# Buffers held until their transfer has landed, a dearer change of array shape, an early table load and an output per tile, in a kernel whose order is planned in Python

## The chip, the cores and the metric

The kernel runs on one core of a Trainium2 chip. The metric is the device time of one execution, in microseconds (us). Before the change the median of three runs is 1993.94 us (1992.65 to 1994.4). One more execution was profiled: it took 1996.48 us, of which the profile's span covers 1994.7 us. Lines such as L372 are lines of the kernel before.

## What is computed

The input is x of shape (4, 1024, 256), float32. It is normalised, and two branches of the normalised xn are added to it:

```python
xn = layernorm(x)
x + attention(xn) + ffn(xn)

# attention: 16 heads of 64, window 64, each query block sees its own and the previous block of keys
h = rms_norm(xn) * gamma
q, k, v = h @ W_qkv                      # 256 -> 3 * 1024
o = softmax(mask(q @ k.T / 8)) @ v
attention = (o * sigmoid(h @ W_gates + b_gates)) @ W_out

# ffn: two layers, 8 heads of 64, window 128
for l in range(2):
    q, k, v = shift_token(x) @ wqkv[l]   # 256 -> 3 * 512
    q, k = rotary(l2norm(q) * qs, l2norm(k) * ks)
    x = x + local_attention(q, k, v) @ wo[l]
    h = layernorm(shift_token(x)) @ w1[l] + b1[l]     # 256 -> 2 * 682
    a, g = split(h)
    x = x + (a * gelu(g)) @ w2[l] + b2[l]
```

shift_token moves the second half of the features one token down. All arithmetic is in float32.

## The kernel before, in words

**Blocks.** The 4096 tokens are cut into 16 blocks of 256 (two tiles of 128). `first_attention(n)` does the normalisation and the 16-head attention of block n, and stores xn (`carried[0]`) and x plus attention (`carried[2]`) to DRAM, L350. `layer(l, n)` fetches a block (L356), does one ffn layer for it, and stores the result for the next layer (L350), or, in the last layer, adds it up and writes the output (L1300). A `layer` is a generator in two halves: the attention half, and, after the `yield`, the feed-forward half, which is recorded `LAG` blocks later.

**The order.** Nothing is issued when it is written down. Each step is recorded with `op(...)`: the engines that could do it with an estimated time on each, a function that issues it, and the buffers that it reads (`r`), writes (`w`) or adds to (`a`). `Plan.run` then plays all recorded steps through a small model of five engines (PE for TensorE, DVE for VectorE, ACT for ScalarE, POOL for GpSimd, SP for the queue that issues most transfers), and `emit` issues them in the order that came out. So the order on every engine is fixed before the chip sees it, and each engine works through its own list strictly in turn. In the model:

- a step's result is ready after its time and a latency, `LAT` (or `lat`), and DVE and POOL times are stretched by `SLACK`;
- each engine picks the step with the smallest score, which is the step's place in the recorded order (`rank`, in us of PE work), plus `IDLE` times the time that the engine would stand idle for it, plus `TURN` where the step has another `mode` than the one before;
- a change of `mode` also takes `SWITCH` us. On PE the mode is the shape in which the 128 x 128 array is used: `full` (128 x 128), `rc` (64 x 64: the score matmuls L711 and L1001, and the second half of the layer's `ob`, L1095) and `c` (128 x 64: `oa`, L779, and the first half of `ob`, L1083). On ACT it is the function table: `exp` or `gelu`;
- steps more than `LOOK` us ahead of the oldest one that is not done are not considered.

**Buffers.** A buffer gets a slot when its first step is planned, out of 92 SBUF slots (`w`), 4 for the gelu (`g`), 40 small ones (`s`) and the 8 banks of PSUM (`ps`). When its last step is planned, the slot becomes free at that step's end plus 0.1 us (L188). For a transfer that end is the end of its issue on SP, not its landing. `spare` keeps some slots of a kind back from steps that run ahead. On the chip, the program's semaphores make the next writer of a slot wait until its last reader has really finished, whatever the plan assumed.

**What each line is.** L385 holds all transposes (by the identity); L584, L677 the first attention's v and q, k; L805 its output projection; L864 the layer's q, k, v; L1114 its output projection; L1246 and L1282 the up and down projections of the feed-forward half. L370 and L372 copy from PSUM to SBUF, on ACT or DVE. L543 normalises twice: `hn` on POOL, which feeds the transposes, and `xn` on DVE, which is stored. L567 scales hT by gamma on ACT, and is the first step there that needs a table. L728 and L1020 are the masked minima of the scores, L738 and L1030 the exponentials, L756 and L1045 the weights, L1259 the gelu, L1266 its product, L1290 the last addition. L932 is the rotation, L361 a power on POOL, L1220 the affine step of the second normalisation.

Of the kernel before, what the change touches and what calls it, by code (L numbers as in the profile page):

```python
# [8 lines left out]
AF = mybir.ActivationFunctionType  # L9
# [32 lines left out]
N_UNIT = 92  # L42
N_GE = 4
N_SMALL = 40
LAG = 3

# [11 lines left out]

class Op:
    __slots__ = (
        "us", "fn", "bufs", "fresh", "mode", "rank", "lat", "left", "ready", "users", "done",
        "start", "end", "eng", "name", "n",
    )


class Plan:
    LAT = {"PE": 0.25, "DVE": 0.3, "ACT": 0.3, "POOL": 0.3, "SP": 2.0}
    SLACK = {"DVE": 1.2, "POOL": 1.2}  # L70
    SWITCH = {"PE": 0.1, "ACT": 1.4}
    TURN = {"PE": 5.0, "ACT": 40.0}
    IDLE = 300.0
    LOOK = 200.0

    def __init__(self, slots, spare):
# [5 lines left out]
    def buf(self, kind):  # L82
        return Buf(kind)

    def op(self, us, fn, r=(), w=(), a=(), mode=None, lat=None, name=""):


        o = Op()
        o.us, o.fn, o.mode, o.lat, o.name = us, fn, mode, lat, name
        o.rank, o.n = self.rank, len(self.ops)  # L90
        if "PE" in us:
            self.rank += us["PE"]
        o.users, o.done, o.ready = [], False, 0.0
        deps = set()
        for b in r:
            deps.update(b.writers)
            b.readers.append(o)
# [12 lines left out]
        o.left = len(deps)  # L110
        self.ops.append(o)
        return o

    def run(self):
        engines = ("PE", "ACT", "DVE", "POOL", "SP")
        at = dict.fromkeys(engines, 0.0)
        mode = dict.fromkeys(engines)
        waiting = {e: [] for e in engines}

        def enter(o):  # L120
            for e in o.us:
                waiting[e].append(o)

        for o in self.ops:
            if not o.left:
                enter(o)
        oldest, out = 0, []

        def begins(o, front):

            need = {}
            for b in o.bufs:
                if b.t is None:
                    need[b.kind] = need.get(b.kind, 0) + 1
            t = o.ready
            for k, n in need.items():
                have = self.free[k]
                keep, slope, most = self.spare[k]
                age = o.rank - front
                if len(have) - n < (min(keep + slope * age, most) if age > 2.0 else 0):  # L140
                    return None
                t = max(t, sorted(f[0] for f in have)[n - 1])
            return t

        while len(out) < len(self.ops):
            while self.ops[oldest].done:
                oldest += 1
            front = self.ops[oldest].rank
            best = None
            for e in engines:  # L150
                picks = []
                for o in waiting[e]:
                    if o.rank > front + self.LOOK:
                        continue
                    t = begins(o, front)
                    if t is None:
                        continue
# [15 lines left out]
            t, _, e, o = best  # L173
            for other in o.us:
                waiting[other].remove(o)
            o.done, o.start, o.end, o.eng = True, t, t + o.us[e] * self.SLACK.get(e, 1.0), e
            at[e] = o.end
            mode[e] = o.mode or mode[e]
            for b in o.bufs:
                if b.t is None:  # L180
                    have = self.free[b.kind]
                    have.sort(key=lambda f: f[0])

                    k = max((i for i, f in enumerate(have) if f[0] <= t), default=0)
                    b.slot = have.pop(k)
                    b.t = b.slot[1]
                b.left -= 1
                b.end = max(b.end, o.end)  # L188
                if not b.left and b.slot is not None:
                    self.free[b.kind].append([b.end + 0.1, b.slot[1]])  # L190
            give = o.end + (self.LAT[e] if o.lat is None else o.lat)
            for u in o.users:
                u.ready = max(u.ready, give)
                u.left -= 1
                if not u.left:
                    enter(u)
            out.append(o)
        self.order = out
# [7 lines left out]
def layers_kernel(  # L206
# [38 lines left out]
            "s": [work.tile([P, 32], F32, name=f"s{n}") for n in range(N_SMALL)],  # L245
            "ps": [psum.tile([P, 512], F32, name=f"ps{n}") for n in range(8)],
        },
        {"w": (4, 0.15, 30), "g": (1, 0.0, 1), "s": (4, 0.05, 12), "ps": (1, 0.02, 3)},
    )
    op, buf = plan.op, plan.buf  # L250

# [1 line left out]
    def fixed(shape, name):  # L253
        return Buf(None, const.tile(shape, F32, name=name))
# [25 lines left out]
        return b.t[:, : k * m * n].rearrange("p (k m n) -> p k m n", k=k, m=m)  # L280

    load_x(0)
    ident = fixed([P, P], "ident")
    load(ident.t, ident_d, ident, eng="ACT")
    gam = fixed([P, NC], "gam")
# [2 lines left out]
    def unit(pieces, us=2.3):  # L288

        u = buf("w")  # L290
        for n, (to, m, of) in enumerate(pieces):

            def bring(e, to=to, m=m, of=of):
                nc.sync.dma_start(u.t[:, to : to + m], of)

            op({"SP": m / 465}, bring, a=(u,), lat=us, name="weights")
        return u


# [48 lines left out]
    def store(dst, src, n):  # L348
        op(
            {"SP": 1.1}, lambda e: nc.sync.dma_start(dst.t, src.t[:, : NT * DIM]),  # L350
            r=(src,), w=(dst,), name="store",
        )

    def fetch(src, b):
# [151 lines left out]
    def first_attention(n, before):  # L506
# [31 lines left out]
            w=(st,), name="scale",  # L538
        )

        def normal(e, to, at):
            for i in range(NT):
                {"DVE": nc.vector, "POOL": nc.gpsimd}[e].tensor_scalar(  # L543
                    v2(to, NT, DIM)[:, i, :], X()[:, i, :], st.t[:, 12 + 2 * i : 13 + 2 * i],
                    st.t[:, at + i : at + i + 1], ALU.subtract, ALU.mult,
                )
# [272 lines left out]
    def layer(l, n, before):  # L819
# [35 lines left out]
        for i in range(NT):  # L855
# [211 lines left out]
            def attend(e, po=po, sTs=sTs, vs=vs, vs_next=vs_next, vt=vt, vt_old=vt_old):  # L1067
# [164 lines left out]
        for m in range(NM):  # L1232
# [39 lines left out]
                op({"DVE": 0.405}, gated, r=(pf, ge, w["b_vec"]), w=(gT[-1],), name="gT")  # L1272
            else:
                op({"DVE": 0.405}, gated, r=(pf, ge, w["b_vec"]), a=(gT[m // 2],), name="gT")
        xo = buf("w")
        for i in range(NT):
            pz = buf("ps")

            def down(e, pz=pz, i=i):
                for m in range(NM):  # L1280
# [7 lines left out]
            op(  # L1288
                {"DVE": 0.345},
                lambda e, pz=pz, i=i: nc.vector.tensor_tensor(  # L1290
                    v2(xo, NT, DIM)[:, i, :], pz.t[:, :DIM], v2(rest, NT, DIM)[:, i, :], ALU.add
                ),
                r=(pz, rest), a=(xo,), name="xo",
            )
# [12 lines left out]
    for n in range(len(blocks)):  # L1307
        if n % NBLK == 0:
# [108 lines left out]
```

## Time and profile before

| What | Value |
|---|---|
| median of three runs | 1993.94 us |
| the profiled execution: time, span | 1996.48 us, 1994.7 us |
| DVE, ACT, POOL busy | 1213.1, 1097.5, 1085.6 us (61%, 55%, 54%) |
| PE weight loads | 1542.5 us (77%), beside the matmuls |
| DMA | 89.36 MB, mean 45 GB/s; 221 GB/s in the first 50 us |
| ACT table loads | 34, of 1283 ns each |
| granted TensorE clock, mean | 0.998 |
| matmul L864 (128 x 512), L1246 (128 x 256), transposes L385 | 593, 380, 275 ns each as modelled |

A row of the timeline reads: start in us, duration in us, engine, line, operation, output <- input, and in brackets how long the engine stood idle before, and what ended that. The duration of a matmul in the records is longer than the distance to the start of the next one, since matmuls overlap: a full-array matmul of 256 columns is 0.38 us long, and the next starts 0.216 us after it. So what a group of matmuls takes is read from its start to the start of the next group. The names in the rows lack buffer numbers: `w` is any SBUF slot, `ps` any bank, `c` a DRAM buffer of `carried`. An SPq row is the issue of a transfer.

### The profile page before, as it was taken

The numbers are of one execution on the slowest core, as the hardware profiler recorded it, in microseconds if no ns is written. First come the engines' busy times: TensorE is split into PE (matmuls) and PEld (weight loads), VectorE is DVE, ScalarE is ACT, GpSimd is POOL, SyncE is SP. The second block draws the span as 40 slices with busy tenths as digits, with TensorE's granted clock in tenths as the row PEclk, the third lists the DMA queues.
The fourth block names the chain that finished last, engine by engine and source line by source line (L and its number), as shares of the span: only waits on it lengthen the run. The fifth ranks groups of instructions, "written<-read, shape, count | busy, mean of one in ns | idle before, by whom it ended". The sixth has DMA issues, their size and how long they took to land.

```text
span 1994.7 us, 50683 instructions
## 1 busy us (share of the span) xinstructions
PE 1953.6 (98%) x18752; PEld 1542.5 (77%) x18752; DVE 1213.1 (61%) x4449; ACT 1097.5 (55%) x3409; POOL 1085.6 (54%) x1697
## 2 busy tenths in 40 slices
PE   7899999999999999999999999999999999999998
PEld 5788888888788677777777777777777777777787
DVE  4444444344344687668677686776767767677662
ACT  4455555446465575655556455564555655556552
POOL 5664456356343786546555475564745646556540
PEclk9999999999999999999999999999999999999999
DMA  7421112111211112301111011110111101111010
GB/s 220 113 54 39 38 44 65 38 44 34 59 34 39 30 31 52 88 20 31 41 28 31 24 49 36 41 37 26 48 39 33 46 22 49 31 41 28 20 28 19
DMA packets 69911, 89.36 MB, mean 45 GB/s; under 512 B 17772, under 2 KB 37792, under 8 KB 69664
## 3 DMA queue, kind: packets, MB, share of 16 engines
q1 hardware_dynamic: 68960, 85.91, 15.9%
q8 instruction: 148, 2.42, 0.5%
q14 instruction: 99, 0.81, 0.1%
q10 hardware_dynamic: 704, 0.21, 0.1%
HBM read 32.61 MB, written 16.78 MB: 25 GB/s over the span
## 4 chain that ended last, share of the span: by engine, by line
PE 91%; DVE 4%; ACT 2%; DMA 1%; issue 1%; POOL 1%; SPq 0%; DVEq 0%; ACTq 0%; POOLq 0%
PE ps L864 16%; PE ps L1246 14%; PE ps L677 11%; PE ps L385 11%; PE ps L1282 8%; PE ps L805 6%; PE ps L584 6%; PE ps L1114 5%; PE ps L1001 4%; PE ps L779 3%; PE ps L1083 3%; PE ps L711 3%; PE ps L1095 2%; DVE w L372 1%; ACT w L370 1%; DMA c<-w 1%
## 5 line engine op out<-in xcount | busy, mean ns | idle before, releaser
L370 ACT COPY w<-ps 128x512 f32<-128x512 f32 (+2 forms) x911 | 428.1, 500 | 600.6 <-PE ps L677 155.0
L372 DVE COPY w<-ps 128x256 f32<-128x256 f32 (+3 forms) x465 | 246.3, 539 | 240.3 <-PE ps L385 110.9
L932 POOL TENSOR_TENSOR w<-w,w 128x256 f32<-128x256 f32 x256 | 234.9, 943 | 284.1 <-ACT w L370 149.9
L864 PE MATMUL ps<-w,w 128*128 128x512 f32 x768 | 352.1, 593 | 1.6 <-DVE w L372 0.9
L1246 PE MATMUL ps<-w,w 128*128 128x256 f32 x1408 | 322.5, 380 | 7.2 <-DVE w L1266 7.2
L1045 POOL TENSOR_SCALAR w<-w,s 128x192 f32<-128x192 f32 x512 | 229.9, 468 | 158.5 <-DVE s L1039 156.5
L385 PEld LDWEIGHTS ps<-ident,w 128*128 128x128 f32 x2112 | 245.9, 141 | 87.4 <-issue 21.7
L385 PE MATMUL ps<-ident,w 128*128 128x128 f32 x2112 | 290.2, 275 | 13.8 <-POOL w L543 9.4
L1246 PEld LDWEIGHTS ps<-w,w 128*128 128x128 f32 x1408 | 260.4, 190 | 45.0 <-ACT w L370 12.0
L756 POOL TENSOR_SCALAR w<-w,s,s 128x128 f32<-128x128 f32 x512 | 223.7, 456 | 110.2 <-DVE s L746 110.0
L361 POOL TENSOR_TENSOR s<-s,mhalf 128x16 f32<-128x16 f32 (+2 forms) x112 | 233.1, 2085 | 76.7 <-DVE s L911 26.7
L1030 ACT ACTIVATE w<-w,s 128x192 f32<-128x192 f32 x512 | 226.0, 445 | 51.2 <-DVE s L1020 49.2
L864 PEld LDWEIGHTS ps<-w,w 128*128 128x128 f32 x768 | 138.3, 190 | 127.5 <-issue 108.7
L677 PE MATMUL ps<-w,w 128*128 128x256 f32 x1024 | 235.6, 380 | 0.0
L738 ACT ACTIVATE w<-w,s 128x128 f32<-128x128 f32 x512 | 197.6, 388 | 28.9 <-DVE s L728 28.9
L677 PEld LDWEIGHTS ps<-w,w 128*128 128x128 f32 x1024 | 188.9, 190 | 25.4 <-ACT w L370 0.8
L1020 DVE CUSTOM_DVE_ANT_0 w<-ps,mask_b,s 128x192 f32<-128x192 f32 x512 | 183.0, 411 | 23.7 <-PE ps L1001 20.2
L1259 ACT ACTIVATE g<-ps,b 128x256 f32<-128x256 f32 x192 | 90.4, 474 | 180.4 <-PE ps L1246 158.5
L728 DVE CUSTOM_DVE_ANT_0 w<-ps,mask_a 128x128 f32<-128x128 f32 x512 | 112.7, 286 | 119.6 <-PE ps L711 102.4
L1282 PE MATMUL ps<-w,w 128*128 128x256 f32 x768 | 171.6, 379 | 2.2 <-ACT w L1220 1.2
L1282 PEld LDWEIGHTS ps<-w,w 128*128 128x128 f32 x768 | 145.6, 190 | 34.5 <-issue 10.1
L1266 DVE SCALAR_TENSOR_TENSOR w<-ps,b,g 128x256 f32<-128x256 f32 x192 | 91.2, 480 | 83.5 <-ACT g L1259 77.0
(75 smaller groups left out, 2584.9 us busy)
## 6 DMA issues: line engine op xcount, KB each, us to landing
w<-w SPq DMA_DIRECT2D x248, 128.0 KB, 2.3
c<-w SPq DMA_DIRECT2D x48, 256.0 KB, 2.0
w<-c SPq DMA_DIRECT2D x48, 256.0 KB, 2.9
w<-in_L_attn_x_dram SPq DMA_DIRECT2D x16, 256.0 KB, 3.2
out_dram<-w SPq DMA_DIRECT2D x16, 256.0 KB, 2.2
w<-w SPq DMA_DIRECT2D x32, 112.0 KB, 2.2
w<-in_L_ffn_w_dram SPq DMA_DIRECT2D x26, 128.0 KB, 2.8
w<-in_L_ffn_wqkv_dram SPq DMA_DIRECT2D x12, 256.0 KB, 3.4
```

The source lines that it names most:

```text
L361: nc.gpsimd.tensor_tensor(dst, src, mhalf.t[:, : src.shape[1]], ALU.pow)
L370: nc.scalar.copy(dst(), src())
L372: nc.vector.tensor_copy(dst(), src())
L385: nc.tensor.transpose(o, i, ident.t)
L677: nc.tensor.matmul(pq.t[:, j * TB : (j + 1) * TB], W[c].t[:, p % GA * P : (p % GA + 1) * P], hT.t[:, c * TB : (c + 1) * TB], start=(c == 0 ...
L756: nc.gpsimd.tensor_scalar(s.t[:, at], s.t[:, at], sm.t[:, 2 * GA + u : 2 * GA + u + 1], gate.t[:, h : h + 1], ALU.mult, ALU.mult,)
L864: nc.tensor.matmul(p.t, y.t[:, at : at + P], w["wqkv"][m][c].t[:, :512], start=(c == 0), stop=(c == NC - 1),)
L932: nc.gpsimd.tensor_tensor(v2(rot, HB, D)[:, :, to], v2(raw[m], HB, D)[:, :, of], v3(sin, 4, 2, D)[:, ti % 4, m, to].unsqueeze(1).to_broadc ...
L1030: nc.scalar.activation(v2(s, 2, WB)[:, u], v2(s, 2, WB)[:, u], AF.Exp, bias=sm.t[:, u : u + 1], scale=-1.0, accum_out=sm.t[:, 2 + u : 3 + u],)
L1045: nc.gpsimd.tensor_scalar(v2(s, 2, WB)[:, u], v2(s, 2, WB)[:, u], sm.t[:, 4 + u : 5 + u], 1.0, ALU.mult, ALU.mult,)
L1246: nc.tensor.matmul(pf.t[:, n_ * TB : (n_ + 1) * TB], wt, d.t[:, c * TB : (c + 1) * TB], start=(c == 0), stop=(c == NC - 1),)
L1282: nc.tensor.matmul(pz.t[:, :DIM], gT[m // 2].t[:, at : at + P], v2(w["w2"][m // 2], 2, DIM)[:, m % 2, :], start=(m == 0), stop=(m == NM - 1),)
```

## The change

It changes numbers and rules of the plan, and three steps:

- a slot that a transfer reads becomes free when the transfer has landed (`give`), not at the end of its issue; stores are given 3.5 us to land; a weight piece is given at least 0.45 us of issue;
- `ob` leaves PE in mode `rc` (its new argument `out`), where the plan took it to leave in `c`;
- other weights: TURN for PE 5 to 30, for ACT 40 to 60; IDLE 300 to 400; LAT of DVE, ACT and POOL 0.3 to 0.4; SLACK 1.2 to 1.25; the slots kept back, of `w` and `ps`; LAG 3 to 4;
- a two-column exponential of zeros, `early`, is recorded ahead of all but the first load, so that ACT loads the `exp` table there;
- `hn` is made on DVE, ahead of `xn`;
- the last layer writes each tile of 128 tokens from a buffer of its own, as soon as it is added up.

```diff
-LAG = 3
+LAG = 4
...
-    LAT = {"PE": 0.25, "DVE": 0.3, "ACT": 0.3, "POOL": 0.3, "SP": 2.0}
-    SLACK = {"DVE": 1.2, "POOL": 1.2}
+    LAT = {"PE": 0.25, "DVE": 0.4, "ACT": 0.4, "POOL": 0.4, "SP": 2.0}
+    SLACK = {"DVE": 1.25, "POOL": 1.25}
     SWITCH = {"PE": 0.1, "ACT": 1.4}
-    TURN = {"PE": 5.0, "ACT": 40.0}
-    IDLE = 300.0
+    TURN = {"PE": 30.0, "ACT": 60.0}
+    IDLE = 400.0
...
+        o.out = out or mode
...
-            mode[e] = o.mode or mode[e]
+            mode[e] = o.out or mode[e]
+            give = o.end + (self.LAT[e] if o.lat is None else o.lat)
...
-                b.end = max(b.end, o.end)
+                b.end = max(b.end, give if e == "SP" else o.end)
                 if not b.left and b.slot is not None:
                     self.free[b.kind].append([b.end + 0.1, b.slot[1]])
-            give = o.end + (self.LAT[e] if o.lat is None else o.lat)
...
-        {"w": (4, 0.15, 30), "g": (1, 0.0, 1), "s": (4, 0.05, 12), "ps": (1, 0.02, 3)},
+        {"w": (4, 0.1, 30), "g": (1, 0.0, 1), "s": (4, 0.05, 12), "ps": (0, 0.02, 3)},
...
     load_x(0)
+
+    early = fixed([P, 2], "early")
+    op({"POOL": 0.1}, lambda e: nc.gpsimd.memset(early.t, 0.0), w=(early,))
+    op(
+        {"ACT": 1.4}, lambda e: nc.scalar.activation(early.t, early.t, AF.Exp), w=(early,),
+        mode="exp", name="early",
+    )
...
-            op({"SP": m / 465}, bring, a=(u,), lat=us, name="weights")
+            op({"SP": max(m / 465, 0.45)}, bring, a=(u,), lat=us, name="weights")
...
-            r=(src,), w=(dst,), name="store",
+            r=(src,), w=(dst,), lat=3.5, name="store",
...
-        op({"POOL": 1.0}, lambda e: normal(e, hn, 24), r=(xb, st), w=(hn,), name="hn")
-        op({"DVE": 0.66}, lambda e: normal(e, xn, 20), r=(xb, st), w=(xn,), name="xn")
+        op({"DVE": 0.66}, lambda e: normal(hn, 24), r=(xb, st), w=(hn,), name="hn")
+        op({"DVE": 0.66}, lambda e: normal(xn, 20), r=(xb, st), w=(xn,), name="xn")
...
                 {"PE": 1.8}, attend, r=(*sTs[0], *sTs[1], vt, vt_old, vs, vs_next), w=po, mode="c",
-                name="ob",
+                out="rc", name="ob",
...
-        xo = buf("w")
+        xo, xos = buf("w"), [buf("w") for _ in range(NT)]
...
+            xi, at = (xo, i) if l < DEPTH - 1 else (xos[i], 0)
...
+            if l == DEPTH - 1:
+                op(
+                    {"SP": 0.6},
+                    lambda e, i=i, xi=xi: nc.sync.dma_start(
+                        out[b, g * TB + i * P : g * TB + (i + 1) * P, :], xi.t[:, :DIM]
+                    ),
+                    r=(xi,), name="out",
+                )
         if l < DEPTH - 1:
             store(carried[l + 1][n], xo, n)
-        else:
-            op(
-                {"SP": 1.1},
-                lambda e: nc.sync.dma_start(
-                    out[b, g * TB : (g + 1) * TB].rearrange("(i p) f -> p i f", p=P),
-                    v2(xo, NT, DIM),
-                ),
-                r=(xo,), name="out",
-            )
```

More of the change, by code (lines that the diff above doesn't have):

```diff
@@ L62 @@
     __slots__ = (
-        "us", "fn", "bufs", "fresh", "mode", "rank", "lat", "left", "ready", "users", "done",
+        "us", "fn", "bufs", "mode", "out", "rank", "lat", "left", "ready", "users", "done",
         "start", "end", "eng", "name", "n",
@@ L83, in buf, with op @@
         return Buf(kind)
-    def op(self, us, fn, r=(), w=(), a=(), mode=None, lat=None, name=""):
+    def op(self, us, fn, r=(), w=(), a=(), mode=None, out=None, lat=None, name=""):
         o = Op()
         o.us, o.fn, o.mode, o.lat, o.name = us, fn, mode, lat, name
+        o.out = out or mode
         o.rank, o.n = self.rank, len(self.ops)
@@ L539, in first_attention, with normal @@
         )
-        def normal(e, to, at):
+        def normal(to, at):
             for i in range(NT):
-                {"DVE": nc.vector, "POOL": nc.gpsimd}[e].tensor_scalar(
+                nc.vector.tensor_scalar(
                     v2(to, NT, DIM)[:, i, :], X()[:, i, :], st.t[:, 12 + 2 * i : 13 + 2 * i],
@@ L1287, in layer @@
             op({"PE": 2.6}, down, r=(*gT, *w["w2"]), w=(pz,), mode="full", name="down")
+            xi, at = (xo, i) if l < DEPTH - 1 else (xos[i], 0)
             op(
                 {"DVE": 0.345},
[L1290 to L1291 removed]
+                lambda e, pz=pz, i=i, xi=xi, at=at: nc.vector.tensor_tensor(
+                    v2(xi, NT, DIM)[:, at, :], pz.t[:, :DIM], v2(rest, NT, DIM)[:, i, :], ALU.add
                 ),
[L1293 removed]
+                r=(pz, rest), a=(xi,), name="xo",
             )
+            if l == DEPTH - 1:
[6 more added lines that the diff above has]
+                )
         if l < DEPTH - 1:
             store(carried[l + 1][n], xo, n)
[L1297 to L1305 removed]
     for n in range(len(blocks)):
```

## The prediction

> **What bounds the kernel now.** I read the page's busy shares and its chain of waits first, then PE's waits, then the timeline wherever PE stood still.
>
> ```profile
> PE 1953.6 (98%) x18752; PEld 1542.5 (77%) x18752; DVE 1213.1 (61%) x4449; ACT 1097.5 (55%) x3409; POOL 1085.6 (54%) x1697
> PE 91%; DVE 4%; ACT 2%; DMA 1%; issue 1%; POOL 1%; SPq 0%; DVEq 0%; ACTq 0%; POOLq 0%
> ```
>
> PE is never done waiting for work to exist, and 91% of the chain lies on it. Beside its own weight loads no engine passes 61%. So an edit pays only in time in which PE does nothing, or does its matmuls further apart. The waits of PE name the first kind (columns: total us, times, longest):
>
> ```profile
> PE ps L385 <- POOL w L543: 9.4, 2, 8.9
> PE ps L1246 <- DVE w L1266: 7.2, 13, 0.6
> PE ps L779 <- ACT w L370: 5.8, 1, 5.8
> PE ps L385 <- DVE s L1020: 3.4, 5, 0.7
> ```
>
> The whole list adds up to 37.1 us: 11.7 us at the start, 5.8 us at one place, and some 20 us in short waits. Each short wait costs about 0.16 us more than its row says, because a matmul is recorded as 0.38 us long where its successor starts after 0.216. With about 30 of them, the short waits are worth some 25 us.
>
> The second kind is seen in PE's timeline in the attention stage:
>
> ```profile
> 235.40 1.89 PE L677 MATMUL ps<-w,w 128*128 128x256 f32 x8
> 237.13 1.04 PE L385 MATMUL ps<-ident,w 128*128 128x128 f32 x8
> 238.09 1.10 PE L711 MATMUL ps<-w,w 64*64 64x128 f32 x32
> 239.13 1.15 PE L779 MATMUL ps<-w,w 128*64 128x64 f32 x32
> 240.21 1.09 PE L385 MATMUL ps<-ident,w 128*128 128x128 f32 x8
> 241.14 3.62 PE L805 MATMUL ps<-w,w 128*128 128x256 f32 x16
> ...
> 245.77 2.85 PE L711 MATMUL ps<-w,w 64*64 64x128 f32 x96
> 248.55 3.72 PE L805 MATMUL ps<-w,w 128*128 128x256 f32 x16
> 252.11 1.04 PE L385 MATMUL ps<-ident,w 128*128 128x128 f32 x8
> 252.98 2.37 PE L584 MATMUL ps<-w,w 128*128 128x272 f32 x8
> ```
>
> Starts tell the price of a change of array shape. Eight transposes in mid-stream take 0.87 us (252.11 to 252.98), before a change 0.96, just after one 0.93: +0.09 to leave the full array, +0.06 to come back to it with a transpose. Sixteen L805 take 3.56 us after a change (248.55 to 252.11) against 16 x 0.216 = 3.45: +0.10 to come back with a matmul. One L711 step takes 1.04 us alone, but three in a row take 2.78; solving the two gives 0.87 per step and 0.17, or, with the like of L779, about 0.15 for each stay in a narrow shape.
>
> **The change, part by part.**
>
> *Fewer changes of shape* (TURN 30, `out`). In the built order of before PE leaves the full array 119 times, comes back 67 times with a matmul and 52 with a transpose, and makes 157 narrow stays (the change inside `ob` is in both kernels and left out). In the changed order: 88, 80, 8 and 106. Before: 119 x 0.09 + 67 x 0.10 + 52 x 0.06 + 157 x 0.15 = 10.7 + 6.7 + 3.1 + 23.6 = 44.1 us. After: 7.9 + 8.0 + 0.5 + 15.9 = 32.3. **Gain 11.8 us**, all on PE. What could give it back: narrow groups bunched together fill PSUM and are drained later; that is in the waits below.
>
> *Slots that transfers read.* The 5.8 us is this:
>
> ```profile
> 67.97 0.38 SPq L350 DMA_DIRECT2D c<-w  x1
> 72.62 1.07 ACT L370 COPY w<-ps 128x512 f32<-128x512 f32 x2 [7.33 <-DMA c<-w]
> 73.25 1.97 PE L779 MATMUL ps<-w,w 128*64 128x64 f32 x32 [5.78 <-ACT w L370]
> 73.00:77.00 4.00, 3.75 (x68) 3.63 (x72) 0.00 (x0) 1.28 (x3) 2.50 (x2) 0.50 0.14 34
> ```
>
> A store of xn stands on SP behind the weights of layer 0; ACT's next copy has been given its slot too early and waits for the landing, and `oa` waits for ACT. The last row is a stage's busy times and, third from the end, PE's clock: 0.50 of full speed. So 3.75 us of matmuls after the gap cost half of that again. The Trainium skill ("TensorE: Matmul & The Clock Gate", the HAM clock gate) says that an idle window of about 3.4 us halves the clock until a busy one has passed. By the wait row alone the place is worth 5.8 us, by the rule and the clock column 5.8 + 1.9 = 7.7; I take 7.7. The same slot fault makes DVE L728 wait 8.0 us for c<-w in four places (up to 2.2 us), each followed by an L584 that PE starts 1.0 to 1.3 us late: 4.7 us. In the order of before, 19 slots with such a last reader are taken again within 1 us of PE work after the transfer's place, 48 within 2; in the changed order none and 2. **Gain 7.7 + 4.7 = 12.4 us.** Other engines' waits for transfers (ACT L897 4.2 us, DVE L1266 3.5) go too; PE hid them, so 0. The longer holding takes slots from steps that run ahead; 92 slots and a lower reserve cover it, and if not, that is a PE wait again (rival 1).
>
> *The start.*
>
> ```profile
> 7.36 2.67 POOL L543 TENSOR_SCALAR w<-w,s 128x256 f32<-128x256 f32 x2 [0.30 <-DVE s L534]
> 10.09 0.69 PE L385 MATMUL ps<-ident,w 128*128 128x128 f32 x2 [0.52 <-POOL w L543]
> 10.85 1.28 ACT L567 ACT_TABLE_LOAD   x1 [10.85 <-PE ps L385]
> ```
>
> On DVE the two halves of `hn` take 0.73 us (its L543 row at 7.17) and end near 8.0 instead of 10.0, so the last transposes start near 8.3: -1.8 us. The table load, 1.28 us, is done by 4 us, under the load of x. First v matmul at 10.0 instead of 13.04. DMA could take this back: the v weights are issued by 5.7 us and land in 3.1 to 6.1, partly behind the two ACT-queue loads that now wait for `early`; PE needs the third pair only some 4 us after its start. SP has nothing new ahead of it. `hn` before `xn` delays the store of xn by 0.7 us, off the path. PE's half clock until 19 us comes from the same gate; by the rule its window runs freely, which may shift the start by 1.7 us either way. **Gain 3.0 us** (1.3 to 4.7). In later blocks `hn` moves 40 us off POOL and about 13 us onto DVE, beside PE: 0.
>
> *Function tables.* The built order has 50 table loads instead of 34. Nearest row: load and next exponential follow each other directly,
>
> ```profile
> 891.04 1.28 ACT L1030 ACT_TABLE_LOAD   x1
> 892.33 0.46 ACT L1030 ACTIVATE w<-w,s 128x192 f32<-128x192 f32 x1
> ```
>
> so 16 more are 20.5 us of ACT. "ScalarE: Activation LUTs" (What ACT_TABLE_LOAD costs) prices a switch at 2.66 us, with a drain of 1.38: 42.6 us. The rows show no drain (888 to 894 us: the gelu before ends at 891.02), so 1.28 holds. ACT is busy 55% and some 66 copies (0.5 us each) come to it from DVE, which makes about 58%; none of before's 34 loads ends a wait of PE. I take 0, bounds 0 and 20.5 lost; no gain is possible.
>
> *Short waits* (LAT, SLACK, IDLE, LAG, spare). About 20 us of the 25 are left after the L584 ones. Longer planned latencies put the reuse of a bank further from its reader: PSUM banks taken again within 1 us of PE work since their last tenant fall from 161 to 124, and `up` banks taken again after one `up` from 61 to 34. How much of it becomes time no row shows. All gone would be -20, and as bad again as now +15. I take a third, nearest to the counts: **-7**.
>
> *Output per tile.* After the last addition stands one transfer (3.1 us to the end); half as large, 2.0 to 2.2 us either way. Gain 0.2. The 16 more issues of 0.45 us on SP stand ahead of the next block's copies (L886), with hidden cost.
>
> Sum: 11.8 + 12.4 + 3.0 + 7 + 0.2 = 34.4 us, so a span of 1994.7 - 34.4 = 1960.3. The profiled execution took 1996.48, 2.5 more than the median 1993.94; from the median, 1959.5. **Predicted: 1960 us**, 1951 to 1971 for this case.
>
> **The rivals.**
>
> 1. *The waits move instead of going.* PE gains only what its own order holds (11.8), the start (3.0) and the tail; where slots or SP queue late, other copies wait. For it: more is held for longer in the same 92 slots, and ACT gets more to do. Against: the counts of slots. 1994 - 15 = 1979 (1972 to 1989).
> 2. *Nearly all short waits go.* For: the tight banks fall by up to 44%. Against: most are between 1 and 2 us apart, as before. 1994 - 47 = 1947.
> 3. *Slower: the exponentials come late.* Between gelu and exp, PE's transposes L385 wait for the chain minimum, exp, weight. If each of the 16 added switches holds PE by more than 34.4 / 16 = 2.15 us, the kernel is slower. At the skill's 2.66 us: 2002. At 1.28, even fully exposed, 1980. Against it: the rows above, and LAG 4 leaves PE other work.
> 4. *The change doesn't hold what it says*: a transfer issued later than planned keeps its 7.7 + 4.7 us: 1972, within the range. For it: the store at 67.97 us stood behind some 40 issues since 37.3 us. Against: issues of weights are now planned at their true 0.45 us.
>
> **How the numbers follow.** Likeliest case 0.60; rival 1 with 4, 0.22; rival 2, 0.09; rival 3, 0.04; something near no change (all gains given back), 0.05. Faster and slower mean by over 0.2%, 4 us, about what a measurement of this kernel can tell. Faster 0.92, same 0.04, slower 0.04. The range runs from 1947 (rival 2) to 1981 (rival 1 in part).
>
> **What would show it.** First v matmul near 10.0 us; no 5.8 us gap of PE and no clock of 0.5 after 20 us; no DVE or ACT wait on c<-w over 1 us; PE's wait list down from 37 to about 17 us; sums of L385, L711, L779 from start to start as above; 50 table loads with no PE wait behind. It would be wrong if PE's list shows one new wait of 3.4 us or more, which the clock doubles, or L385 <- POOL L1045 with more than 10 us.

## The result and the profile after

The changed kernel takes 1958.05 us (median of four runs, 1957.2 to 1958.31) against 1993.57 us (median of four, 1992.65 to 1994.4) for the kernel before on the same chip: a ratio of 0.9821, with a 95% interval of 0.9804 to 0.9838. Its profiled execution took 1958.31 us, with a span of 1956.5 us, 38.2 less than the profiled execution of before; that one was 2.9 us slower than its median, so the spans differ by more than the 35.5 us of the medians. The forecast was 1960 us.

From here on a line number of the kernel after is that of before plus 8 in the steps that matter: the transposes L385 are L393, the copies L370 and L372 are L378 and L380, and so on. The page's busy shares and its chain of waits, after:

```profile
PE 1936.3 (99%) x18752; PEld 1537.4 (79%) x18752; DVE 1183.6 (60%) x4426; ACT 1151.4 (59%) x3481; POOL 1034.6 (53%) x1666
PE 96%; DVE 1%; ACT 1%; POOL 1%; DMA 0%; SPq 0%; issue 0%; DVEq 0%; ACTq 0%; POOLq 0%
```

TensorE's part of the chain rose from 91 to 96%: what was removed is time in which it stood still. ACT came to 59% (58% was forecast). PE's waits (total us, times, longest):

```profile
PE ps L393 <- DVE w L551: 7.7, 1, 7.7
PE ps L1254 <- DVE w L1274: 1.7, 3, 0.6
PE ps L1009 <- ACT w L378: 1.2, 2, 1.1
PE ps L1290 <- ACT w L1228: 1.2, 1, 1.2
PE ps L1290 <- DVE w L1274: 1.1, 1, 1.1
PE ps L592 <- DMA w<-in_L_attn_W_qkv_dram: 0.9, 1, 0.9
```

The list now adds up to 16.6 us in 17 entries, from 37.1 in 34; 8.6 of them are the start. The 5.8 us for ACT's copy are gone, and the thirteen waits for L1274 (formerly L1266) are three. The last row is of a new kind: at the start PE waits 0.9 us for a piece of the v weights. The stretch in which the clock had been at 0.50 (busy time of PE, PE weight loads, DVE, ACT, POOL; then PE's clock, DMA share, GB/s):

```profile
73.00:77.00 4.00, 4.00 (x130) 3.80 (x131) 2.83 (x27) 3.02 (x14) 0.00 (x0) 1.00 0.77 207
```

PE is busy throughout, at full clock. The start on PE's timeline, where before had v matmuls from 13.04 and q and k matmuls from 23.30 us:

```profile
7.68 1.12 PE L393 MATMUL ps<-ident,w 128*128 128x128 f32 x4 [7.68 <-DVE w L551]
9.73 9.00 PE L592 MATMUL ps<-w,w 128*128 128x272 f32 x24 [0.93 <-DMA w<-in_L_attn_W_qkv_dram]
18.57 7.72 PE L685 MATMUL ps<-w,w 128*128 128x256 f32 x35
```

The first v matmul comes 3.3 us earlier, the first q, k matmul 4.7 us: the v matmuls between (12 of them, 24 records: a float32 matmul leaves two in these rows) took 10.26 us before and 8.84 now. In the attention stage narrow work now stands together:

```profile
224.74 2.69 PE L719 MATMUL ps<-w,w 64*64 64x128 f32 x92
227.36 7.17 PE L813 MATMUL ps<-w,w 128*128 128x256 f32 x32
234.37 1.04 PE L393 MATMUL ps<-ident,w 128*128 128x128 f32 x8
```

After this the array stays full until 259.24 us; before, it changed for two narrow groups of 32 at 238.09 us and again for narrow work at 245.77.

Where the 38.2 us come from, measured from start to start of PE's groups (the first term by counting changes in the order):

| Term | Forecast | Measured |
|---|---|---|
| changes of array shape | 11.8 | 11.8 (counts times the prices of the prediction; start to start, all changes together took 44.0 us before and 33.1 after, 10.9 less) |
| the 5.8 us place and its half clock | 7.7 | 7.7 |
| short waits (4.7 + 7) | 11.7 | 12.9 (27.0 to 14.1 us after 78 us) |
| start | 3.0 | 4.7 |
| end | 0.2 | 0.45 |
| table loads | 0 | 0 |
| not assigned | | 0.65 |

This table says where time went, not which edit took it away. That is what the experiments are for.

### The profile page after: what moved, and what is told of

Its sections match the earlier page's. It is cut to its first block, busy times and chain, and to the rows that moved or that the text cites. A ratio compares the mean times of both kernels' runs of the same rounds, so it can differ in the third digit from the quotient of the medians.

```text
span 1956.5 us, 50660 instructions
## 1 busy us (share of the span) xinstructions
PE 1936.3 (99%) x18752; PEld 1537.4 (79%) x18752; DVE 1183.6 (60%) x4426; ACT 1151.4 (59%) x3481; POOL 1034.6 (53%) x1666
## 4 chain that ended last, share of the span: by engine, by line
PE 96%; DVE 1%; ACT 1%; POOL 1%; DMA 0%; SPq 0%; issue 0%; DVEq 0%; ACTq 0%; POOLq 0%
PE ps L872 16%; PE ps L1254 15%; PE ps L685 11%; PE ps L393 11%; PE ps L1290 9%; PE ps L1122 6%; PE ps L592 6%; PE ps L813 6%; PE ps L1009 5%; PE ps L1091 3%; PE ps L787 3%; PE ps L719 3%; PE ps L1103 2%; ACT w L378 1%; DVE w L380 1%; POOL w L1053 0%
## 5 line engine op out<-in xcount | busy, mean ns | idle before, releaser
L378 ACT COPY w<-ps 128x512 f32<-128x512 f32 (+2 forms) x976 | 468.0, 503 | 577.4 <-PE ps L685 154.6
L380 DVE COPY w<-ps 128x256 f32<-128x256 f32 (+2 forms) x400 | 203.7, 515 | 259.4 <-PE ps L393 144.6
L393 PEld LDWEIGHTS ps<-ident,w 128*128 128x128 f32 x2112 | 253.0, 141 | 104.8 <-issue 53.6
L393 PE MATMUL ps<-ident,w 128*128 128x128 f32 x2112 | 293.7, 273 | 8.1 <-DVE w L551 7.7
L1053 POOL TENSOR_SCALAR w<-w,s 128x192 f32<-128x192 f32 x512 | 239.0, 485 | 107.8 <-DVE s L1047 101.4
L369 POOL TENSOR_TENSOR s<-s,mhalf 128x16 f32<-128x16 f32 (+2 forms) x112 | 241.8, 2160 | 98.4 <-DVE s L919 43.7
L940 POOL TENSOR_TENSOR w<-w,w 128x256 f32<-128x256 f32 x256 | 209.4, 842 | 110.6 <-ACT w L378 60.1
L1028 DVE CUSTOM_DVE_ANT_0 w<-ps,mask_b,s 128x192 f32<-128x192 f32 x512 | 187.2, 412 | 27.6 <-PE ps L1009 20.0
L1274 DVE SCALAR_TENSOR_TENSOR w<-ps,b,g 128x256 f32<-128x256 f32 x192 | 88.7, 478 | 85.0 <-ACT g L1267 77.2
```

Of the source, the lines that this page charges most:

```text
L369: nc.gpsimd.tensor_tensor(dst, src, mhalf.t[:, : src.shape[1]], ALU.pow)
L378: nc.scalar.copy(dst(), src())
L380: nc.vector.tensor_copy(dst(), src())
L393: nc.tensor.transpose(o, i, ident.t)
L940: nc.gpsimd.tensor_tensor(v2(rot, HB, D)[:, :, to], v2(raw[m], HB, D)[:, :, of], v3(sin, 4, 2, D)[:, ti % 4, m, to].unsqueeze(1).to_broadc ...
L1053: nc.gpsimd.tensor_scalar(v2(s, 2, WB)[:, u], v2(s, 2, WB)[:, u], sm.t[:, 4 + u : 5 + u], 1.0, ALU.mult, ALU.mult,)
```

## The experiments

Theory: the sum of the prediction, that is, each edit acts by its own mechanism. Rivals: the gain of short waits belongs to something else (the order that TURN makes, or the longer latencies), the parts need each other, or the table loads cost something that another edit pays for. The reserves, the issue time of weights and the output per tile were not run singly, and TURN and `out` were not parted. The columns: median and range, the ratio to the kernel before on the same chip with its interval, and the distance from before's median of that chip. The change is 35.5 us below before. It was not run again on the chips of these rows, where the medians of before are 0.6 to 1.3 us above 1993.57; so a distance from the change, below, is good to about 1 us.

| Run | Median (range), us | Ratio [95%] | us |
|---|---|---|---|
| e1: before, hold alone | 1983.77 (1983.57 to 1985.21) | 0.9948 [0.9935, 0.996] | -10.9 |
| e2: before, TURN alone | 1971.23 (1970.89 to 1971.67) | 0.9883 [0.9869, 0.9896] | -23.5 |
| e3: before, start alone | 1991.45 (1989.52 to 1993.23) | 0.9983 [0.9976, 0.999] | -3.2 |
| e4: after, without hold | 1962.58 (1961.85 to 1963.05) | 0.9839 [0.9825, 0.9852] | -32.1 |
| e5: after, 114 table loads | 2017.4 (2016.01 to 2018.21) | 1.0116 [1.0101, 1.0131] | +23.3 |
| e6: after, TURN undone | 1991.09 (1988.63 to 1997.33) | 0.9988 [0.9981, 0.9994] | -3.1 |
| e7: after, old latencies | 1960.35 (1960.15 to 1961.38) | 0.9831 [0.9817, 0.9846] | -33.8 |
| e8: after, LAG 3 | 1961.02 (1960.36 to 1962.12) | 0.9834 [0.9818, 0.9851] | -33.1 |
| e9: after, one table load | 1958.35 (1957.37 to 1959.31) | 0.9819 [0.9803, 0.9836] | -36.5 |
| e10: before, one table load | 1994.53 (1992.22 to 1995.73) | 0.9998 [0.9989, 1.0006] | -0.3 |
| e11: after, warmed clock | 1956.38 (1956.07 to 1958.91) | 0.9812 [0.9797, 0.9826] | -38.5 |
| e12: before, three parts | 1971.94 (1970.06 to 1973.61) | 0.9886 [0.9872, 0.9901] | -22.9 |

The medians of before were 1994.69 us (e1 to e4), 1994.14 (e5 to e8) and 1994.86 (e9 to e12).

### e1: the hold alone, in the order of before

```diff
-                b.end = max(b.end, o.end)
+                b.end = max(b.end, give if e == "SP" else o.end)
...
+            r=(src,), w=(dst,), lat=3.5, name="store",
```

Slots were held until the landing; the other weights of the plan, and with them PE's order, stayed.

> The kernel before with one part of the change: a slot read by a transfer becomes free in the plan at the landing, stores given 3.5 us. The order on PE is the same as before, only slots differ. My theory (each part pays by itself): the 5.8 us wait of L779, the half clock after it and the four late L584 go, 12.4 us, so about 1981. Rival 1 (waits move): another copy waits instead, 1990 to 1994.

Measured: 10.9 us less. The place at 73 us (windows, columns as above; line numbers of before):

```profile
67.00:73.00 6.00, 6.00 (x104) 5.37 (x99) 3.80 (x33) 4.67 (x21) 0.00 (x0) 1.00 0.47 158
73.00:77.00 4.00, 4.00 (x21) 3.51 (x20) 0.83 (x4) 2.54 (x14) 3.80 (x4) 1.00 0.58 195
```

PE no longer stands still, and its clock is 1.00. In PE's waits the 5.8 us row is gone, and so are the late L584 behind L372 and L728 (3.2 and 0.8 us before); no engine waits for a landing of c<-w or out_dram<-w any more. What is new is the second of these, at 79.55 us, and other short waits are as before:

```profile
PE ps L1246 <- DVE w L1266: 7.3, 13, 0.9
PE ps L385 <- POOL w L756: 1.2, 1, 1.2
```

So the mechanism of the hold is shown: it takes away the waits for landings, the gap and its half clock. Of the 12.4 us, 1.2 came back as a wait for L756, which makes the weights of the softmax.

### e4: the change without the hold

```diff
-                b.end = max(b.end, give if e == "SP" else o.end)
+                b.end = max(b.end, o.end)
```

The order on PE is the same as in the change.

> The changed kernel without the holding of slots until the landing; the order on PE is the same as in the changed kernel, 23 slots are taken again within 1 us of PE work after a transfer instead of none. My theory: waits for c<-w and out<-w come back and reach PE in part, as in the kernel before: 6 to 14 us slower than the changed kernel, 1964 to 1972. Rival: in this order the copies behind are hidden, within 2 us of 1958, and the 12.4 us of before belonged to its order alone.

Measured: 4.5 us more than the change. The waits for transfers are back on other engines:

```profile
ACT w L378 <- DMA out_dram<-w: 20.9, 8, 6.1
ACT w L378 <- DMA c<-w: 15.8, 10, 1.8
DVE w L380 <- DMA c<-w: 6.2, 12, 0.5
```

ACT stands 36.7 us behind landings (2.6 us in the change), once for 6.1 us, and yet the time grows by only 4.5 us. PE's own list grew only from 16.6 to 17.1 us; from start to start, 2.7 us more lie in pauses of less than 0.1 us where PE goes on to another line, too short for a row. In this order PE mostly doesn't need what stands behind those copies at once. So the hold is worth 10.9 us in the old order and 4.5 in the new one.

### e2: TURN and `out` alone

```diff
-    TURN = {"PE": 5.0, "ACT": 40.0}
+    TURN = {"PE": 30.0, "ACT": 40.0}
...
-                name="ob",
+                out="rc", name="ob",
```

> The kernel before with TURN for PE 30 and ob leaving in rc, nothing else. Its built order leaves the full array 91 times, comes back 89 times with a matmul and 2 with a transpose, and makes 106 narrow stays: 33.1 us at the prices of the prediction against 44.1, and it has 62 table loads. My theory: 11 us less from the shapes, short waits unchanged within 7 us: 1983, 1976 to 1990. Rival 3 (table loads cost 1.28 us each on PE's path): 28 more loads, 36 us, so slower than before.

Measured: 23.5 us less, twice what the shapes give. In its order the changes of shape are worth 11.0 us less by the prices of the prediction. The rest is waits: those between 30 and 85 us fell from 6.2 to 2.2 us (the 5.8 us place is not there in this order, though its slots are not held; a pause of 1.49 us is left at 73.76, for which the profile names no releaser), its half clock (1.9 us) went with it, and the short waits after 655 us fell from 21.9 to 11.8 us. Near the end something was lost (a wait of PE, then a window around it; lines are those of before plus 1):

```profile
PE ps L386 <- DVE w L1198: 3.1, 1, 3.1
```

```profile
1945.00:1953.00 8.00, 6.37 (x18) 4.77 (x19) 1.60 (x5) 1.49 (x3) 0.00 (x0) 0.57 0.00 1
```

A single wait of 3.1 us brought the clock to 0.57 over these 8 us. So my reading of TURN as a matter of shapes alone fell. TURN and `out` were changed together, here and in e6. The plan worked out without the chip, but with one of the two alone, leaves the full array 94 times with TURN 30 and 118 times with `out`, against 91 with both and 119 with neither: the order is TURN's in the main; no run times them apart.

### e6: TURN undone in the change

```diff
-    TURN = {"PE": 30.0, "ACT": 60.0}
+    TURN = {"PE": 5.0, "ACT": 60.0}
...
-                out="rc", name="ob",
+                name="ob",
```

> The changed kernel with TURN for PE back at 5 and ob planned as leaving in c. Its order leaves the full array 120 times, comes back 69 times with a matmul and 51 with a transpose, 153 narrow stays: 43.7 us against 32.3. My theory: 11.4 us slower by the shapes, plus some short waits (banks taken again within 1 us of PE work: 201 instead of 124): 1969 to 1977, likeliest 1972. Rival: TURN mostly set short waits, then 1980 or more, as e2 gained 23 us from it alone.

Measured: 33 us more than the change, which leaves almost nothing of its gain. Shapes 11.4 us by counts and prices (8.9 from start to start); from start to start, short waits after 655 us 15, between 85 and 655 us 3.8, and a half clock at 658.8 to 665.6 us 3.4; together 33.6, against 32.3 in the spans. PE's waits, then PE's row ahead of the half clock, and the window with it:

```profile
PE ps L393 <- ACT w L378: 6.8, 10, 1.1
PE ps L393 <- DVE w L380: 5.1, 6, 2.2
PE ps L1091 <- ACT w L378: 2.7, 4, 0.7
PE ps L872 <- ACT w L378: 1.5, 2, 0.8
```

```profile
658.23 1.42 PE L393 MATMUL ps<-ident,w 128*128 128x128 f32 x8 [2.20 <-DVE w L380]
658.00:666.00 8.00, 6.92 (x18) 3.84 (x19) 4.44 (x10) 5.68 (x19) 8.00 (x13) 0.57 0.00 0
```

Here a wait of 2.20 us was enough to halve the clock. PE waits for the copies out of PSUM, L378 and L380, which stand with 16.1 us in these four rows. In the change L378 stands in PE's list with some 2.5 us. The number of PSUM banks that are taken again within 1 us of PE work since the last PE step of their last tenant goes along with it:

| Kernel | Banks taken again within 1 us | PE's waits after 655 us, us |
|---|---|---|
| e6 | 201 | 27.5 |
| before | 161 | 21.9 |
| e8 | 135 | 15.6 |
| e2 | 132 | 11.8 |
| e12 | 126 | 14.0 |
| after | 124 | 12.6 |
| e7 | 112 | 12.2 |

The two orders with TURN 5 (e6, before) have the most of both. Among the five with TURN 30 nothing goes along, and e2, e8 and e12 contain a single wait of 2.8 to 3.13 us near the end. So the counts fit the view that with TURN 30 PE's steps come in an order in which a bank is asked for later; they don't show it, and no run changed the banks alone.

### e7: the old latencies in the change

```diff
-    LAT = {"PE": 0.25, "DVE": 0.4, "ACT": 0.4, "POOL": 0.4, "SP": 2.0}
-    SLACK = {"DVE": 1.25, "POOL": 1.25}
+    LAT = {"PE": 0.25, "DVE": 0.3, "ACT": 0.3, "POOL": 0.3, "SP": 2.0}
+    SLACK = {"DVE": 1.2, "POOL": 1.2}
...
-    IDLE = 400.0
+    IDLE = 300.0
```

> The changed kernel with LAT 0.3, SLACK 1.2 and IDLE 300 as before. Shapes 32.9 us (against 32.3), 60 table loads, banks taken again within 1 us of PE work 112. My theory of the prediction (longer planned latencies take a third of the short waits): 7 us slower, 1965. Rival: the short waits went with TURN, whose order has fewer of them, and the latencies do nothing: 1956 to 1961.

Measured: 2.3 us more than the change. In the profiled execution 1.4 of its 3.1 us of added span lie in the v matmuls of the start (10.21 us instead of 8.84), the waits after 655 us are not longer (12.2 against 12.6), and fewer banks are taken again soon (112 against 124). So the 7 us that the prediction gave to latencies, LAG and reserves are not a gain of LAT, SLACK and IDLE here.

### e8: LAG 3 in the change

```diff
-LAG = 4
+LAG = 3
```

> The changed kernel with LAG 3. Shapes 30.8 us (against 32.3), 58 table loads, slots taken again within 2 us of PE work after a transfer 1. Theory: LAG gives PE more work to choose from and so hides waits; without it 0 to 8 us slower, likeliest 1960. Rival: it does nothing, 1956 to 1959.

Measured: 3.0 us more. It has the same place near the end as e2 (a wait of PE, then the window):

```profile
PE ps L393 <- DVE w L1205: 3.0, 2, 2.8
```

```profile
1935.00:1943.00 8.00, 6.38 (x18) 4.83 (x19) 1.47 (x5) 1.49 (x3) 0.00 (x0) 0.57 0.00 0
```

With LAG 3 PE has nothing else to do while the last second-half block is normalised: it waits for it for 2.8 us, and then works at half clock. In the change no row of PE's waits after the start has a longest one above 1.2 us. The place is in each order with TURN 30 and LAG 3 (e2, e8, e12). It is in none with LAG 4, and in none with TURN 5.

### e12: three parts together

Before, with the hold, TURN (PE 30, ACT 60) with `out`, and `early` with `hn` on DVE; LAT, SLACK, IDLE, LAG, reserves, issue times of weights and the output as before. Two details differ from the single runs: TURN for ACT was 40 in e2, and in e3 the plan still counted `hn` as a step of POOL.

```diff
-    TURN = {"PE": 5.0, "ACT": 40.0}
+    TURN = {"PE": 30.0, "ACT": 60.0}
...
-                b.end = max(b.end, o.end)
+                b.end = max(b.end, give if e == "SP" else o.end)
```

> The kernel before with three parts of the change: slots held until landing, TURN and the true exit of ob (with TURN for ACT 60), early table with hn on DVE; LAT, SLACK, IDLE, LAG, the reserves, the weights' issue time and the output as before. Shapes 33.8 us, 60 loads, banks taken again within 1 us 126. If the parts carry the change and the retuned weights are worth the 2 to 3 us that e7 and e8 showed: 1960 to 1964. If the weights are needed together: 1966 or more.

Measured: 22.9 us less than before, 13.9 more than the change. The three parts alone are worth 10.9, 23.5 and 3.2, together 37.6 us. The timeline near the end, and PE's window there; then two windows around 700 us:

```profile
1943.70 1.11 DVE L1205 TENSOR_SCALAR w<-w,s 128x128 f32<-128x128 f32 x4 [1.19 <-DMA out_dram<-w]
1944.10 1.41 PE L393 MATMUL ps<-ident,w 128*128 128x128 f32 x4 [3.13 <-DVE w L1205]
```

```profile
1943.00:1951.00 8.00, 5.75 (x15) 4.26 (x16) 1.11 (x4) 1.49 (x3) 0.29 (x1) 0.57 0.02 6
697.80:701.23 3.43, 1.86 (x12) 1.28 (x13) 3.00 (x9) 3.43 (x11) 3.43 (x6) 1.00 0.00 0
701.23:704.64 3.41, 3.41 (x6) 1.61 (x7) 2.05 (x4) 0.97 (x2) 3.41 (x3) 0.50 0.03 5
```

DVE's normalisation starts behind the landing of an output, PE waits 3.13 us for DVE, and the clock halves. Of DVE's 1.19 us the landing is a small part: the power on POOL that it also needs ends at 1943.29, 0.41 us before. This is the place of e8, where PE waits 2.77 us with no landing involved. Around 700 us no wait is long: PE waits 1.06, 0.47 and 0.28 us within 2.3 us, is busy for 1.86 us of the 3.43 in the upper row, and the next 3.41 us run at half clock. From start to start, the profiled spans of e12 and the change (11.8 us apart) differ by 4.4 us of half clock, 2.8 of PE's waits ahead of 655 us and 1.1 at the start; the rest is spread over pauses too short for a row. So the remaining weights do count, once the three parts are in. Which of them keeps PE out of such places was not settled: LAG (e8) and the latencies (e7) undone singly cost only 3.0 and 2.3.

### e3: the start alone

```diff
+    early = fixed([P, 2], "early")
...
-                {"DVE": nc.vector, "POOL": nc.gpsimd}[e].tensor_scalar(
+                nc.vector.tensor_scalar(
```

`hn` is issued on DVE, but the plan still counts it as a step of POOL, so PE's order is that of before.

> The kernel before with the early exponential and with hn issued on DVE, in the order of before (hn ahead of xn, plan otherwise unchanged). The prediction's step: first v matmul at 10.0 instead of 13.04 us, 3.0 us less, 1990.6. The changed kernel's trace says more: its PE clock is full from 13.3 us instead of 19.0, and its L685 begins 4.7 us earlier, so 4.7 us less, 1988.9. If the clock's window is a matter of chance, the start of the full clock lies between 12 and 17 us here.

Measured: 3.2 us less (median of 18 runs). The timeline (lines of before plus 7):

```profile
9.81 9.28 PE L591 MATMUL ps<-w,w 128*128 128x272 f32 x24 [0.93 <-DMA w<-in_L_attn_W_qkv_dram]
18.92 7.07 PE L684 MATMUL ps<-w,w 128*128 128x256 f32 x32
```

The first v matmul is early by the same 3.2 us. What the v matmuls then take differs within one and the same start: with the old start it was 10.26, 9.96, 9.51 and 9.16 us in four profiled executions (before, e10, e1, e2), and with the new one 8.84 to 10.21 (after, e7). It depends on when the clock becomes full: after 19.14, 18.59, 17.62 and 16.88 us in the first four, after 12.94 and 15.72 in the last two. At full clock throughout they take 7.26 us (e11, below); 7.26 us plus half of the time from the first v matmul to the full clock gives each of the six within 0.05 us.

### e5, e9, e10: the table loads

In e5 a two-column gelu stood ahead of every eighth exponential of a layer, unknown to the plan: 114 loads instead of 50.

```diff
+            count[0] += 1
+            if count[0] % 8 == 0:
+                nc.scalar.activation(early.t, early.t, AF.Gelu)
```

> The changed kernel in its own order on every engine, but before every 8th exponential step of the layers ACT computes a gelu of the two-column early tile, whose result is not used: 114 table loads instead of 50, 82 us more of loads on ACT, each pair just ahead of an exponential. My theory (loads are covered, 0 on PE's path): within 8 us of the changed kernel, 1958 to 1966. Rival 3 at 1.28 us per load on PE's path: 2040; at the skill's 2.66 us: 2128; each pair delaying PE once by 2.6 us: 32 x 2.6 = 83, again 2041.

Measured: 59 us more than the change, 0.93 us for each of the 64 added loads. One of them on ACT, and the matmul that comes late for it (lines are those of after plus 1):

```profile
691.54 1.28 ACT L1040 ACT_TABLE_LOAD   x1
692.84 0.20 ACT L1040 ACTIVATE early<-early 128x2 f32<-128x2 f32 x1
693.06 1.28 ACT L1042 ACT_TABLE_LOAD   x1
695.86 1.60 PE L1010 MATMUL ps<-w,w 64*64 64x192 f32 x32 [4.03 <-ACT w L379]
```

```profile
PE ps L394 <- ACT w L379: 24.6, 27, 2.7
PE ps L1010 <- ACT w L379: 6.5, 3, 4.0
```

In its two largest rows PE doesn't wait for the exponentials, as rival 3 thought, but for copies out of PSUM (L379, which is L378 of after) that stand on ACT behind the switch. Each load takes 1.28 us, and in these rows ACT idles 0.02 us or less around it. Four of PE's waits, of 4.03, 2.74, 2.20 and 2.53 us, were followed by 3.41 us of half clock each, so part of the 59 us is the clock's.

In e9 and e10 the gelus are computed as exponentials, in after and in before; so nothing is loaded but the first table. In the rows the two take the same time (473 ns each for 128 x 256).

```diff
-AF.Gelu
+AF.Exp
```

> The changed kernel with an exponential computed in place of the gelu, so that one table load is left of 50; every other instruction and its place are the same. It measures what the 49 loads cost in this order. My prediction's value (planned loads are covered): 0, so 1957 to 1959. From e5, where 64 unplanned loads cost 59 us: 0.93 us each would be 45 us, 1913. Half-way: planned loads cost something, 1 to 10 us.

> The same replacement of the gelu by an exponential in the kernel before: 1 load instead of 34. If loads are covered there too, 1994; at 0.93 us each 1963. If loads cost the changed kernel more than the kernel before, e9 gains more against the changed kernel than this does against the kernel before.

Measured: 1958.35 us and 1994.53 us, as with all loads (1958.05 for the change; 1994.86 for before on that chip). So the 49 later loads of the change and the 33 of before, which the plan knows and puts where nothing is urgent, cost nothing that can be measured (the doubt is about 1 us), and 64 that it doesn't know cost 0.93 us each. The first load of before, at 10.85 us, stays in e10: it is part of the start.

### e11: a warmed clock

Fourteen matmuls of zeros by 128 columns, issued ahead of everything else on PE, while x is on its way:

```diff
+    for _ in range(14):
+        nc.tensor.matmul(bank[:, :P], warm, warm, start=True, stop=True)
```

> The changed kernel with 14 matmuls of zeros (128 columns, into a bank not in use) on PE ahead of the first transposes, in the 7 us in which PE has nothing to do. The kernel's own work and order are the same. If the half clock until 13.3 us is what the gate makes of an idle PE, the clock is full before the first v matmul at 9.7 us, 3.6 us of half rate go, and the kernel gains 1.8 us: 1956.2. Rival: the clock's rise is set by time since the launch; then 13.3 us stays and the time is 1958 or a little more.

Measured: 1956.38 us. The timeline of PE (each of the 14 leaves two records):

```profile
0.98 5.42 PE L1349 MATMUL ps<-warm 128*128 128x128 f32 x28 [0.98 <-POOL mhalf L334]
9.32 7.42 PE L592 MATMUL ps<-w,w 128*128 128x272 f32 x24 [0.93 <-ACT w L575]
16.58 3.62 PE L685 MATMUL ps<-w,w 128*128 128x256 f32 x16
```

The first q, k matmul starts at 16.58 us instead of 18.57; the v matmuls take 7.26 us, at full clock from the first on (the clock is full from 5.26 us). The span is 2.6 us below that of the change, the median 1.7. It is the fastest kernel of this study. Its interval overlaps the change's, so the runs alone don't separate the two; the rows of the start do. So the half clock of the start is of the idle PE ahead of it, and not of the time since the launch, the rival that was put down.

## Why the prediction was right, and where its steps were not

**The time** (1960 forecast, 1958.05 measured) lies in the likeliest case, and the sum holds term by term in the trace (the table above). But two terms were put down to the wrong edit, and what a part is worth depends on the others. That the total came out within 2 us all the same is luck to that extent: the trace's terms are right, the account of which edit makes them is not.

**Shapes, 11.8 us.** Right in the trace (10.9 from start to start), and by counts and prices e2 (11.0) and e6 (11.4) have the same term. The step that was mis-sized is the sentence "Gain 11.8 us, all on PE. What could give it back: narrow groups bunched together fill PSUM and are drained later". Bunching didn't give anything back; it took waits away as well: TURN alone is worth 23.5 us (e2), and undoing it costs 33 (e6). The counts of banks that I put beside the latencies are set mostly by TURN: with the old latencies they are lower still (e7).

**Slots that transfers read, 12.4 us.** The mechanism is right: e1 has 10.9 of it, full clock at the place, and no waits for landings on c<-w. As a part of this change it is 4.5 us (e4), because 12.4 was worked out in the order of before, and the order of TURN passes that place without a gap even if the slots are not held (e2). The sign "no DVE or ACT wait on c<-w over 1 us" missed narrowly: one of 1.1 us is left on ACT, and ACT waits 1.5 us and DVE 1.2 for an output.

**Start, 3.0 us.** First v matmul at 9.73 us where I had 10.0. The trace has 4.7 us and e3's runs 3.2: about 1.4 us of the 4.7 is the moment at which the clock became full, which differs between executions. In that the trace's size is chance. The caution about v weights was right in kind: 0.9 us of wait for them.

**Function tables, 0.** Right (e9, e10). One sentence on the way was not: "none of before's 34 loads ends a wait of PE". The first one lies in PE's wait of 2.26 us before 13.04 us, and its removal is counted under the start. What made the 0 right was not only that the loads lie off PE's path: 1.28 us rows with free time on ACT held in e5 too, and there each cost 0.93 us. They lie off the path because the plan counts them and puts them where no copy is urgent. The larger price that the prediction set against the rows, with a drain, is not seen in the rows of these runs.

**Short waits, 7 us beside the 4.7.** The size held (12.9 against 11.7 in all); the reason "longer planned latencies" did not (e7: 2.3 us, some of which is the start). The step that failed is "I take a third, nearest to the counts": the waits went with TURN (e2, e6). What LAG does is another thing than I said: in an order with TURN 30 it leaves PE work at the end, and so keeps one wait of 2.8 us and its half clock away (e8).

**Adding up.** Alone, the three parts give 37.6 us, together only 22.9 (e12), with all the rest 35.5. The prediction added terms from one order, as if an edit of the plan left the order of the others alone. This is also where its rivals stood: e12 shows a part of rival 1 (waits move instead of going), and the change, with the weights that e12 leaves out, doesn't have those waits.

**Still open:** wait by wait, which buffers TURN relieves; what `out` does beside TURN; and which of the remaining weights (reserves, the issue time of weights and the output per tile were not tried singly) closes the gap between e12 and the change.

## What to carry to other kernels

In a kernel whose order is planned, price an edit in the order that it makes, and test it both ways: alone in the old kernel, and taken out of the new one; here one part was worth 10.9 or 4.5 us, another 23.5 or 33. Hold a buffer in the plan until the transfer that reads it has landed, and tell the plan of table loads: what the plan knows was hidden, what it didn't know cost 0.93 us a load. When the matmul engine is 98% busy, look for its changes of array shape from start to start, and for waits of 2 us and more, single or close together: where the clock halved after them, they cost about 1.4 to 2.5 times their row here.

## What the runs showed of the chip

- Single waits of PE of 2.20 us (e6), 2.77 (e8) and 3.13 (e2, e12) halved the clock, and so did three of 1.06, 0.47 and 0.28 us close together (e12). The Trainium skill ("TensorE: Matmul & The Clock Gate", What's actually happening) speaks of an idle window of about 3.4 us, from which the prediction took 3.4 us as the wait to fear; here much less idle time was enough. Single waits of up to 1.2 us in the change after its start, and of up to 1.68 us in e5, left the clock at 1.00.
- Inside a kernel a half clock lasted 3.41 us (e3, e5, e12 at 701 us) or 6.83 us (before, e2, e6, e8, e10, e12 near the end), and in each of the traces its changes lie whole multiples of 3.41 us apart. So one such wait costs up to 1.7 or 3.4 us beside its own row.
- The moment of full clock after the start differs between executions of the same start: the v matmuls took 8.84 to 10.21 us with the new start, and 7.26 us behind matmuls of zeros (e11). So up to 1.4 us between two executions are not of the code that is compared.
- A table load is 1.28 us with 0.02 us or less of idle time on either side in the rows shown, also where 64 of them stand in the way (e5).
